# Moving a layer norm's statistics into the stage ahead of it, and re-ordering the projection stage of an attention layer

## The chip, the cores and the metric

The kernel runs on one core of a Trainium2 chip. The metric is the device time of one execution, in microseconds (us).

## The reference, cut to what matters

An image of 256 channels and 64 x 64 pixels goes through two layers. Layer 0 normalizes groups of channels, computes a linear attention whose sums over windows are taken with an integral image (window sizes 64, 32 and 16), projects it and adds the input. Layer 1 sees the 4096 pixels as tokens of 256 channels: softmax attention with 8 heads over normalized tokens, then a mixture of experts (top 2 of 8).

```python
x = x + L0_conv(_gn(x), Wq, Wk, Wv, Wout, bout)
t = _to_tokens(x)                                   # 4096 x 256
t = t + L1_attn(_ln_t(t), w_qkv, b_qkv, w_out, b_out)
t = t + L1_ffn(_ln_t(t), Wr, br, ln_g, ln_b, W1, b1, W2, b2)

def _ln_t(v, eps=1e-5):                             # the norm that the change moves
    m = mean(v, -1); s = var(v, -1)
    return (v - m) / sqrt(s + eps)
```

The change concerns the end of layer 0, and of layer 1 the first norm and the products q, k and v.

## The kernel before

All tokens stay on the chip in `t`, 32 tiles of 128 tokens by 256 channels, with 8 more columns for the router. The image is cut into 8 strips (`NCH` = 8), each of `NB` = 4 tiles: strip or chunk c holds the tiles 4c to 4c+3.

**The end of layer 0.** The function `attend` runs for each half of the channels (g = 0, 1), and in it for each window in the order (1, 0, 2). The last window of the second half (w = 2, r = 1) goes over the 8 strips. A strip has up to six steps, alternately 384 and 512 columns wide. A step makes scores for four heads on TensorE (L738) into four PSUM banks out of six that rotate (tag `sc`, `bufs=6`). `masked` then multiplies them by masks into SBUF: VectorE does it straight from PSUM (L568), and for head 1, in every other step for head 3 too, ScalarE copies (L564) and GpSimd multiplies (L568). Two steps later the masked scores go against v (L754). A score bank comes free when VectorE's multiply or ScalarE's copy has read it, and the next step's scores of heads 2 and 3 go into the banks that this step's heads 0 and 1 had. After a strip's last step VectorE multiplies the sum by the reciprocals (L769), and two steps later, in the third step of the next strip, `projection` makes the output product (L641) in two of the rotating banks and VectorE adds it to `t` (L645), two tiles at a time. With that add the strip's four tiles of layer 1's input are final.

**The start of layer 1.** The weights `wqkv` come by DMA on SyncE's queue (L863), the bias rows on ScalarE's (L866, L867). For a chunk the kernel takes the statistics of four tiles (`stats`: L801, L802), adds epsilon and takes the root (`begin`: L806 on VectorE, L807 on ScalarE), inverts it (`end`: L810), normalizes each tile to `hn` (L926), turns it on TensorE (L816) and copies it to `act` (`to_channels`, L817). Then come 8 products for q and k, 512 wide (L947), on each of which VectorE adds the bias (L951) and takes the largest absolute value (L952), and 8 products for v (L958), biased by VectorE (L965) and with the router's columns copied by ScalarE (L966). GpSimd adds the output bias to `t` (L936). The first two chunks' statistics and the small products `biases` and `router` are placed by hand. PSUM has four rotating banks here (`psum("a_ps0", 4)`).

After the last chunk a bound on the scores is worked out from the largest values (L988 to L1003), every engine reads its verdict `tame` (L1004) and branches, and the attention begins with L1074. Each engine runs its own instructions in order; what the order is, a scheduler of the framework decides from the program's order and priorities.

Of the kernel before, what the change touches and what calls it, by code (L numbers as in the profile page):

```python
# [34 lines left out]
NT = N // P  # L35
CH = 512
NCH = N // CH
# [3 lines left out]
NB = IMG // BH  # L41
# [5 lines left out]
NE = 8  # L47
# [5 lines left out]
TAME = 60.0  # L53
# [58 lines left out]
def tile_conv_attn_hybrid(ctx: ExitStack, tc: tile.TileContext, a: dict, out: bass.AP):  # L112
    nc = tc.nc

    const = ctx.enter_context(tc.tile_pool(name="const", bufs=1))
    keep = ctx.enter_context(tc.tile_pool(name="keep", bufs=1))

    def psum(name, bufs):
        return tc.tile_pool(name=name, bufs=bufs, space=PSUM)
# [9 lines left out]
    cst = constants_of("", const)  # L129
    ident = cst["ident"]  # L130
# [5 lines left out]

    wr_sum = keep.tile([P, NE], F32, name="wr_sum")
    act = keep.tile([P, KC, N], F32, name="act")

    def tok(i):  # L140
        return slice(P * i, P * (i + 1))
# [44 lines left out]
    with ExitStack() as phase:  # L186
# [28 lines left out]
        with (  # L215
# [58 lines left out]
            for i in range(0, NCH, 2):  # L274
                for k in range(KC):
# [5 lines left out]
                        op0=ALU.subtract,  # L281
# [311 lines left out]
        def attend(g, work, ps, qk, v, ssum, rec, woT):  # L593
# [34 lines left out]
            for w in windows:  # L628
# [8 lines left out]
                def projection(ix, raw=raw, w=w):  # L637
                    for b in range(0, NB, 2):
                        po = score().rearrange("p (i o) -> p i o", o=C)
                        for i in range(2):  # L640
                            nc.tensor.matmul(  # L641
                                po[:, i, :], raw[:, ix, tok(b + i)], woT[:, w, :], start=True, stop=True
                            )
                        to = t[:, NB * ix + b : NB * ix + b + 2, :C]
                        nc.vector.tensor_add(to, po, to)  # L645

# [140 lines left out]
            with tc.tile_pool(name="c_work", bufs=1) as work, psum("c_ps2", 1) as ps:  # L787
                attend(g, work, ps, *of)

    class Norm:  # L790


        def __init__(self, pool, name):
            self.pool = pool
            self.mv = pool.tile([P, NT, 2], F32, name=f"{name}_mv")
            self.rstd = pool.tile([P, NT], F32, name=f"{name}_rstd")
            self.mean, self.var = self.mv[:, :, 0], self.mv[:, :, 1]

        def stats(self, i):
            st6 = self.pool.tile([P, 6], F32, tag="st6", name="st6", bufs=2)  # L800
            nc.vector.bn_stats(st6, t[:, i, :C])  # L801
            nc.vector.bn_aggr(self.mv[:, i, :], st6)  # L802

        def begin(self, first, last):

            nc.vector.tensor_scalar_add(self.rstd[:, first:last], self.var[:, first:last], 1e-5)  # L806
            nc.scalar.sqrt(self.rstd[:, first:last], self.rstd[:, first:last])  # L807

        def end(self, first, last):
            nc.vector.reciprocal(self.rstd[:, first:last], self.rstd[:, first:last])  # L810

    def to_channels(src, dst, ps):

        tp = ps.tile([P, CH], F32, tag="mm", name="ps_mm")
        for k in range(KC):
            last = nc.tensor.transpose(tp[:, tok(k)], src[:, tok(k)], ident)  # L816
        nc.scalar.copy(dst, tp[:, :C].rearrange("p (k n) -> p k n", k=KC))  # L817
        return last
# [20 lines left out]
    with ExitStack() as phase:  # L839
# [15 lines left out]
        with (  # L855
            tc.tile_pool(name="a_in", bufs=1) as win,
            tc.tile_pool(name="a_ln", bufs=2) as work,
            psum("a_ps0", 4) as ps,
        ):

            wqkv = win.tile([P, KC, 3 * C + NE], F32, name="wqkv")
            wr = wqkv[:, :, 3 * C :]
            nc.sync.dma_start(wqkv[:, :, : 3 * C], a["L1_attn_w_qkv"].rearrange("(k p) o -> p k o", p=P))  # L863
            nc.sync.dma_start(wr, a["L1_ffn_Wr"].rearrange("(k p) e -> p k e", p=P))
            rows6 = win.tile([6, P], F32, name="bias_rows")
            nc.scalar.dma_start(rows6[:4], a["L1_attn_b_qkv"][: 2 * C].rearrange("(m p) -> m p", p=P))  # L866
            nc.scalar.dma_start(rows6[4:], a["L1_attn_b_out"].rearrange("(m p) -> m p", p=P))  # L867
            bo = row_on_all("L1_attn_b_out", C, win)
            bv = win.tile([P, C], F32, name="bv")
            nc.scalar.dma_start(bv, a["L1_attn_b_qkv"][2 * C :].partition_broadcast(P))  # L870
# [4 lines left out]
            def biases():  # L875
                tp = ps.tile([P, CH], F32, tag="mm", name="ps_mm")
                nc.tensor.transpose(tp[:, :6], rows6, ident[:6, :6])
                nc.vector.tensor_copy(bqk, tp[:, :6])
# [30 lines left out]
                        )  # L909
                nc.vector.tensor_copy(wo[:, :, C:], tp[:, : KC * NE].rearrange("p (k e) -> p k e", e=NE))  # L910

            norm = Norm(small, "ln1")

            def begin(c):
                for i in range(NB * c, NB * (c + 1)):
                    norm.stats(i)
                norm.begin(NB * c, NB * (c + 1))

            begin(0)
            for c in range(NCH):  # L920
                if 0 < c < NCH - 1:
                    begin(c + 1)
                norm.end(NB * c, NB * (c + 1))
                for i in range(NB * c, NB * (c + 1)):
                    hn = work.tile([P, C], F32, name="hn", bufs=4)
                    last = nc.vector.tensor_scalar(  # L926
                        hn,
                        t[:, i, :C],
                        norm.mean[:, i : i + 1],
                        norm.rstd[:, i : i + 1],  # L930
                        op0=ALU.subtract,
                        op1=ALU.mult,
                    )
                    turned = to_channels(hn, act[:, :, tok(i)], ps)

                    nc.gpsimd.tensor_add(t[:, i, :C], t[:, i, :C], bo)  # L936
                if c == 0:

                    with tc.issue_after(last.ins), tc.issue_after(turned.ins):
                        biases()  # L940
                        begin(1)
                for s in range(2):
                    for g in range(KC):
                        m = KC * s + g
                        pr = ps.tile([P, CH], F32, tag="mm", name="ps_mm")
                        for k in range(KC):
                            nc.tensor.matmul(  # L947
                                pr, wqkv[:, k, tok(m)], act[:, k, chunk(c)], start=k == 0, stop=k == KC - 1
                            )
                        to = qk[:, s, g, chunk(c)]  # L950
                        nc.vector.tensor_scalar_add(to, pr, bqk[:, m : m + 1])  # L951
                        nc.vector.tensor_reduce(  # L952
                            peak[:, s, g, c : c + 1], to, AX.X, ALU.max, apply_absolute_value=True
                        )
                for i in range(NB * c, NB * (c + 1)):
                    pv = ps.tile([P, CH], F32, tag="mm", name="ps_mm")
                    for k in range(KC):
                        product = nc.tensor.matmul(  # L958
                            pv[:, : C + NE],
                            act[:, k, tok(i)],  # L960
                            wqkv[:, k, 2 * C :],
                            start=k == 0,
                            stop=k == KC - 1,
                        )
                    biased = nc.vector.tensor_add(v[:, i, :], pv[:, :C], bv)  # L965
                    nc.scalar.copy(t[:, i, C:], pv[:, C : C + NE])  # L966
                if c == 0:
                    with tc.issue_after(biased.ins), tc.issue_after(product.ins):
                        router()
                if c == 2:  # L970
                    expert_columns(win, ps)
# [15 lines left out]
            top = small.tile([P, 2, KC], F32, name="top")  # L987
            nc.vector.tensor_reduce(top, peak, AX.X, ALU.max)  # L988
            most = small.tile([P, KC, 4], F32, name="most")
            nc.vector.tensor_mul(  # L990
                most,
                cst["head"].unsqueeze(1).to_broadcast([P, KC, 4]),
                top[:, 0].unsqueeze(2).to_broadcast([P, KC, 4]),
            )
            nc.vector.tensor_mul(most, most, top[:, 1].unsqueeze(2).to_broadcast([P, KC, 4]))
            tp = ps.tile([P, CH], F32, tag="mm", name="ps_mm")
            nc.tensor.matmul(
                tp[:1, : 4 * KC], ones[:, :1], most.rearrange("p g h -> p (g h)"), start=True, stop=True
            )
            bound = small.tile([1, 1], F32, name="bound")  # L1000
            nc.vector.tensor_reduce(bound, tp[:1, : 4 * KC], AX.X, ALU.max)
            tame = small.tile([1, 1], mybir.dt.int32, name="tame")
            nc.vector.tensor_scalar(tame, bound, TAME / C**-0.5, None, op0=ALU.is_le)  # L1003
        tame = nc.values_load(tame[:1, :1], min_val=0, max_val=1)  # L1004

        attnT = act
# [639 lines left out]
```

## Time and profile before

| what | value |
|---|---|
| time before | 2807.0 us, median of 3 runs (2806.38 to 2809.07) |
| the profiled execution | 2808.7 us, its span 2806.9 us |
| TensorE busy, share of the span | 2661.7 us, 95% |
| VectorE, ScalarE, GpSimd busy | 1879.4, 1489.9, 813.6 us |
| the last window of layer 0, second half | about 907 to 1003.3 us of the span |
| norm, q, k and v of layer 1 | 1003.3 to 1113.7 us of the span |

The span is what the profiler saw from the first to the last instruction; the execution's time is 1.8 us longer. The profile is of one execution. Times in the views are microseconds from the span's start. TensorE's matmuls are pipelined, so "busy" on it means that some matmul was in flight.

### The profile page before, as it was taken

To read this page: it belongs to the slowest core of one execution; us is meant where nothing else is said; L and a number is where in the kernel's file an instruction comes from. 1 tells how busy PE (TensorE), PEld (TensorE's weight loads), DVE (VectorE), ACT (ScalarE), POOL (GpSimd) and SP (SyncE) were. 2 spreads that over 40 slices of the span, in tenths; PEclk is the share of its full clock that TensorE was granted. 3 is DMA by queue.
4 is the path that set the end of the run, shared out by engine and by line. 5 is a ranking of instruction groups with operands and counts; after the bars stand their busy time and mean duration, and the time that the engine had idled before them with its cause. 6 is when DMAs were issued, how large, how long until landed. Compare 5 with 4: busy or idle time off the path is not lost.

```text
span 2806.9 us, 72020 instructions
## 1 busy us (share of the span) xinstructions
PE 2661.7 (95%) x31078; PEld 1217.1 (43%) x31078; DVE 1879.4 (67%) x2476; ACT 1489.9 (53%) x2060; POOL 813.6 (29%) x914
## 2 busy tenths in 40 slices
PE   6889999998999989999999999999999689999996
PEld 5454336645433655111212121222222168888884
DVE  6758688575878886888888888888888721111114
ACT  3222323222232312999898989898999622222222
POOL 2057777305777831000000000000000022222220
PEclk9999999999999999999999999999999879999997
DMA  5000000000000000555555555555555356656665
GB/s 143 6 23 26 10 28 21 8 0 23 28 7 32 17 21 1 106 110 121 109 116 110 117 110 120 110 111 110 118 108 120 86 186 214 197 196 197 205 216 190
DMA packets 120044, 264.97 MB, mean 94 GB/s; under 512 B 20099, under 2 KB 81129, under 8 KB 105637
## 3 DMA queue, kind: packets, MB, share of 16 engines
q0 software_dynamic: 22368, 133.18, 22.4%
q1 hardware_dynamic: 90168, 118.15, 12.9%
q10 hardware_dynamic: 7180, 8.93, 0.9%
q8 instruction: 248, 4.06, 0.6%
q14 instruction: 80, 0.65, 0.1%
HBM read 126.76 MB, written 18.12 MB: 52 GB/s over the span
## 4 chain that ended last, share of the span: by engine, by line
PE 92%; DVE 3%; issue 2%; DMA 2%; ACT 1%; POOL 0%; SPq 0%; ACTq 0%; DVEq 0%; POOLq 0%
PE ps_three L1074 18%; PE ps_acc L1033 18%; PE ps_hp L1552 9%; PE ps_yp L1561 8%; PE ps_sc L738 8%; PE ps_acc L754 7%; PE ps_sc L641 3%; PE ps_sc L665 3%; PE ps_acc L696 3%; PE ps_mm L947 2%; PE ps_two L329 2%; PE ps_two L362 2%; PE ps_two L443 1%; PE ps_acc L684 1%; PE ps_mm L958 1%
## 5 line engine op out<-in xcount | busy, mean ns | idle before, releaser
L1074 PE MATMUL ps_three<-qk 32*64 32x512 f32 x6144 | 564.0, 613 | 3.3 <-DVE t L983 1.8
L1074 PE MATMUL ps_one<-qk 32*64 32x512 f32 x2048 | 557.5, 613 | 1.4 <-ACT pe L1083 1.4
L1105 DVE TENSOR_TENSOR act<-act,pe 128x2048 f32<-128x2048 f32 x195 | 446.8, 2292 | 97.2 <-ACT pe L1086 62.9
L564 ACT COPY sm<-ps_sc 128x384 f32<-128x384 f32 (+3 forms) x454 | 218.5, 511 | 531.0 <-PE ps_sc L738 345.8
L1086 ACT ACTIVATE pe<-ps_three 128x1536 f32<-128x1536 f32 x330 | 476.9, 1445 | 0.0
L568 DVE TENSOR_TENSOR sm<-ps_sc,mask 128x512 f32<-128x512 f32 (+3 forms) x740 | 340.1, 519 | 70.2 <-PE ps_sc L738 66.9
L568 POOL TENSOR_TENSOR sm<-sm,mask 128x192 f32<-128x192 f32 (+3 forms) x428 | 350.1, 848 | 111.9 <-ACT sm L564 111.5
L1105 DVE TENSOR_TENSOR act<-act 128x2048 f32<-128x2048 f32 x150 | 343.8, 2292 | 55.7 <-ACT act L1086 42.5
L1094 POOL DMA_DIRECT2D pe<-pe x108 | 93.1, 862 | 953.7 <-ACT pe L1086 652.2
L1033 PE MATMUL ps_acc<-pe,v 128*32 128x512 f32 x2640 | 352.4, 606 | 0.0
L1555 ACT ACTIVATE hid<-ps_hp,cols 128x256 f32<-128x256 f32 (+1 forms) x288 | 133.2, 462 | 360.2 <-PE ps_hp L1552 359.1
L1074 PEld LDWEIGHTS ps_three<-qk 32*64 32x64 f32 x6144 | 112.7, 130 | 416.5 <-ACT pe L1083 243.2
L1086 ACT ACTIVATE act<-ps_three 128x1536 f32<-128x1536 f32 x182 | 263.2, 1446 | 0.0
L1552 PE MATMUL ps_hp<-xe,w 128*128 128x256 f32 (+1 forms) x1152 | 246.8, 371 | 0.0
L1561 PE MATMUL ps_yp<-w,hid 128*128 128x256 f32 x1088 | 240.8, 379 | 0.0
L738 PE MATMUL ps_sc<-qk 32*64 32x384 f32 (+3 forms) x3584 | 232.4, 458 | 0.0
L1083 ACT ACTIVATE pe<-ps_one 128x512 f32<-128x512 f32 x330 | 197.4, 598 | 59.4 <-PE ps_one L1074 35.7
L568 POOL TENSOR_TENSOR sm<-sm,ycut 128x384 f32<-128x384 f32 (+4 forms) x146 | 147.5, 1031 | 252.3 <-ACT sm L564 252.0
L1552 PEld LDWEIGHTS ps_hp<-xe,w 128*128 128x128 f32 x1152 | 201.2, 190 | 39.5 <-ACT hid L1555 5.3
L1561 PEld LDWEIGHTS ps_yp<-w,hid 128*128 128x128 f32 x1088 | 204.2, 190 | 26.4
L754 PE MATMUL ps_acc<-sm,v 128*32 128x256 f32 (+3 forms) x2688 | 213.2, 419 | 0.1
L1531 DVE TENSOR_SCALAR xe<-ps_tp,cols 128x256 f32<-128x256 f32 (+1 forms) x72 | 34.8, 525 | 238.9 <-PE ps_tp L1527 217.2
(253 smaller groups left out, 3006.8 us busy)
## 6 DMA issues: line engine op xcount, KB each, us to landing
pe<-pe POOLq DMA_DIRECT2D x108, 1024.0 KB, 7.4
w<-in_L_ffn_W SPq DMA_DIRECT2D x72, 1024.0 KB
by<-recs SPq DMA_DIRECT2D x48, 256.0 KB
b<-in_L_ffn_b SPq DMA_DIRECT2D x36, 128.0 KB
rows<-in_x SPq DMA_DIRECT2D x16, 256.0 KB
zrows<-act SPq DMA_DIRECT2D x4, 1024.0 KB
y<-yrows ACTq DMA_DIRECT2D x8, 512.0 KB
y<-yrows SPq DMA_DIRECT2D x8, 512.0 KB
```

The source lines that it names most:

```text
L564: nc.scalar.copy(sm[:, :used], sc[:, :used])
L568: done = engine.tensor_mul(to, of, mk.unsqueeze(1).to_broadcast(list(to.shape)))
L738: nc.tensor.matmul(scs[h][u : u + rows, at : at + n], kT[hs[h], P * i + u : P * i + u + rows], qT[hs[h], CH * ix + CELL * c0 : CH * ix + C ...
L754: nc.tensor.matmul(acc[hs[h], CELL * c0 : CELL * c1], v[:, i, hs[h]], sms[h][:, at : at + n], start=not begun[0], stop=last and at == plac ...
L1033: nc.tensor.matmul(to[D * hd : D * (hd + 1), :], lhsT(hd), rhs(hd), start=start, stop=stop, skip_group_check=True,)
L1074: nc.tensor.matmul(to[CELL * u : CELL * (u + 1), :], qk[hs, 1, g, P * i + CELL * u : P * i + CELL * (u + 1)], qk[hs, 0, g, chunk(qc)], sta ...
L1083: first = nc.scalar.activation(head(pe, 0), one, AF.Exp, scale=C**-0.5)
L1086: nc.scalar.activation(pe[:, CH:], three.rearrange("p h n -> p (h n)"), AF.Exp, scale=C**-0.5).ins
L1105: latest[:] = [nc.vector.tensor_add(total, total, weights_of[r, i]).ins]
L1552: nc.tensor.matmul(hp[:, :n], w1[:, k, tok(m)], x_now[:, k, :n], start=k == 0, stop=k == KC - 1)
L1555: nc.scalar.activation(hid[:, m, :n], hp[:, :n], AF.Gelu, bias=cols[:, m : m + 1])
L1561: nc.tensor.matmul(yp, hid[:, m, tok(j)], w2[:, m, :], start=m == 0, stop=m == NH - 1)
```

## The change

It does four things.

1. The class `Norm` moves up, and `norm1` is made before layer 0. In the last window of the second half, `projection` of the strips 0 to 6 takes the statistics of each tile right after the add to `t`, and calls `begin` for its chunk and `end` for the one before. After strip 6 chunk 0 is also normalized, into columns of `act` that layer 0 has done with (`first_rows`). Chunk 7's statistics are taken in layer 1.
2. In layer 1 each chunk is normalized and turned (`turn(c + 1)`) between the q, k products and the v products of the chunk before it; `turn(0)` runs at the start. PSUM has eight rotating banks instead of four.
3. ScalarE adds the biases of q and k (`activation` with `Identity`) where VectorE did. A small `Exp` is called on ScalarE ahead of the loop. The two bias rows' DMAs go ahead of the weights on SyncE's queue instead of following `wo` on ScalarE's.
4. The bound (`bounds`) is worked out before the last two tiles' v products instead of after them.

```diff
+    norm1 = Norm(keep, "ln1")
+    first_rows = lambda i: act[:, KC - 1, N - C * (i + 1) : N - C * i]
...
                         to = t[:, NB * ix + b : NB * ix + b + 2, :C]
                         nc.vector.tensor_add(to, po, to)
+                        if g == KC - 1 and w == windows[-1] and ix < NCH - 1:
+                            for i in range(2):
+                                norm1.stats(NB * ix + b + i)
+                    if g == KC - 1 and w == windows[-1] and ix < NCH - 1:
+                        if ix:
+                            norm1.end(NB * (ix - 1), NB * ix)
+                        norm1.begin(NB * ix, NB * (ix + 1))
+                        if ix == NCH - 2:
+                            for i in range(NB):
+                                norm1.apply(first_rows(i), i)
...
-            psum("a_ps0", 4) as ps,
+            psum("a_ps0", 8) as ps,
...
+            nc.sync.dma_start(rows6[:4], a["L1_attn_b_qkv"][: 2 * C].rearrange("(m p) -> m p", p=P))
+            nc.sync.dma_start(rows6[4:], a["L1_attn_b_out"].rearrange("(m p) -> m p", p=P))
             nc.sync.dma_start(wqkv[:, :, : 3 * C], ...)
...
-                        nc.vector.tensor_scalar_add(to, pr, bqk[:, m : m + 1])
+                        nc.scalar.activation(to, pr, AF.Identity, bias=bqk[:, m : m + 1])
...
+            turn(0)
+            biases()
+            root = small.tile([1, 1], F32, name="root")
+            nc.scalar.activation(root, ident[:1, :1], AF.Exp)
+            for c in range(NCH):
+                queries_keys(c)
+                if c + 1 < NCH:
+                    turn(c + 1)
+                if c == 0:
+                    norm.end(NT - 2 * NB, NT - NB)
+                if c == 1:
+                    for i in range(NT - NB, NT):
+                        norm.stats(i)
+                    norm.begin(NT - NB, NT)
+                if c == 2:
+                    norm.end(NT - NB, NT)
                 for i in range(NB * c, NB * (c + 1)):
+                    if i == NT - 2:
+                        bounds()
+                    biased, product = values(i)
```

More of the change, by code (lines that the diff above doesn't have):

```diff
@@ L138, in tile_conv_attn_hybrid, with __init__, stats, begin @@
     act = keep.tile([P, KC, N], F32, name="act")
+    class Norm:
+        def __init__(self, pool, name):
+            self.pool = pool
+            self.mv = pool.tile([P, NT, 2], F32, name=f"{name}_mv")
+            self.rstd = pool.tile([P, NT], F32, name=f"{name}_rstd")
+            self.mean, self.var = self.mv[:, :, 0], self.mv[:, :, 1]
+        def stats(self, i):
+            st6 = self.pool.tile([P, 6], F32, tag="st6", name="st6", bufs=2)
+            nc.vector.bn_stats(st6, t[:, i, :C])
+            nc.vector.bn_aggr(self.mv[:, i, :], st6)
+        def begin(self, first, last):
+            nc.vector.tensor_scalar_add(self.rstd[:, first:last], self.var[:, first:last], 1e-5)
+            nc.scalar.sqrt(self.rstd[:, first:last], self.rstd[:, first:last])
+        def end(self, first, last):
+            nc.vector.reciprocal(self.rstd[:, first:last], self.rstd[:, first:last])
+        def apply(self, to, i):
+            nc.vector.tensor_scalar(
+                to,
+                t[:, i, :C],
+                self.mean[:, i : i + 1],
+                self.rstd[:, i : i + 1],
+                op0=ALU.subtract,
+                op1=ALU.mult,
+            )
+    norm1 = Norm(keep, "ln1")
+    first_rows = lambda i: act[:, KC - 1, N - C * (i + 1) : N - C * i]
     def tok(i):
@@ L788, in tile_conv_attn_hybrid @@
                 attend(g, work, ps, *of)
[L790 to L810, printed above, removed]
     def to_channels(src, dst, ps):
@@ L862, in tile_conv_attn_hybrid @@
             wr = wqkv[:, :, 3 * C :]
+            rows6 = win.tile([6, P], F32, name="bias_rows")
+            nc.sync.dma_start(rows6[:4], a["L1_attn_b_qkv"][: 2 * C].rearrange("(m p) -> m p", p=P))
+            nc.sync.dma_start(rows6[4:], a["L1_attn_b_out"].rearrange("(m p) -> m p", p=P))
             nc.sync.dma_start(wqkv[:, :, : 3 * C], a["L1_attn_w_qkv"].rearrange("(k p) o -> p k o", p=P))
             nc.sync.dma_start(wr, a["L1_ffn_Wr"].rearrange("(k p) e -> p k e", p=P))
[L865 to L867 removed]
             bo = row_on_all("L1_attn_b_out", C, win)
@@ L910, in router, with turn, queries_keys @@
                 nc.vector.tensor_copy(wo[:, :, C:], tp[:, : KC * NE].rearrange("p (k e) -> p k e", e=NE))
-            norm = Norm(small, "ln1")
-            def begin(c):
+            norm = norm1
+            def turn(c):
                 for i in range(NB * c, NB * (c + 1)):
[L916 to L934, printed above, removed]
+                    hn = work.tile([P, C], F32, name="hn", bufs=4) if c else first_rows(i)
+                    if c:
+                        norm.apply(hn, i)
+                    to_channels(hn, act[:, :, tok(i)], ps)
                     nc.gpsimd.tensor_add(t[:, i, :C], t[:, i, :C], bo)
[L937 to L941, printed above, removed]
+            def queries_keys(c):
                 for s in range(2):
@@ L954, in tile_conv_attn_hybrid, with values @@
                         )
-                for i in range(NB * c, NB * (c + 1)):
[L956 to L966, printed above, removed]
+            def values(i):
+                pv = ps.tile([P, CH], F32, tag="mm", name="ps_mm")
+                for k in range(KC):
+                    product = nc.tensor.matmul(
+                        pv[:, : C + NE],
+                        act[:, k, tok(i)],
+                        wqkv[:, k, 2 * C :],
+                        start=k == 0,
+                        stop=k == KC - 1,
+                    )
+                biased = nc.vector.tensor_add(v[:, i, :], pv[:, :C], bv)
+                nc.scalar.copy(t[:, i, C:], pv[:, C : C + NE])
+                return biased, product
@@ new lines, in tile_conv_attn_hybrid, with bounds @@
+            tame = small.tile([1, 1], mybir.dt.int32, name="tame")
+            def bounds():
+                top = small.tile([P, 2, KC], F32, name="top")
+                nc.vector.tensor_reduce(top, peak, AX.X, ALU.max)
+                most = small.tile([P, KC, 4], F32, name="most")
+                nc.vector.tensor_mul(
+                    most,
+                    cst["head"].unsqueeze(1).to_broadcast([P, KC, 4]),
+                    top[:, 0].unsqueeze(2).to_broadcast([P, KC, 4]),
+                )
+                nc.vector.tensor_mul(most, most, top[:, 1].unsqueeze(2).to_broadcast([P, KC, 4]))
+                tp = ps.tile([P, CH], F32, tag="mm", name="ps_mm")
+                nc.tensor.matmul(
+                    tp[:1, : 4 * KC], ones[:, :1], most.rearrange("p g h -> p (g h)"), start=True, stop=True
+                )
+                bound = small.tile([1, 1], F32, name="bound")
+                nc.vector.tensor_reduce(bound, tp[:1, : 4 * KC], AX.X, ALU.max)
+                nc.vector.tensor_scalar(tame, bound, TAME / C**-0.5, None, op0=ALU.is_le)
@@ L983, in tile_conv_attn_hybrid @@
             nc.vector.tensor_add(t[:, :, C:], t[:, :, C:], shift)
[L987 to L1003, printed above, removed]
         tame = nc.values_load(tame[:1, :1], min_val=0, max_val=1)
```

## The prediction

> **What bounds the kernel now.** I read the page first: TensorE is busy for 95% of the span, and the chain that ended last is 92% TensorE. The change touches two stages, so I cut them out: the windows of busy time (time, then PE, PEld, DVE, ACT, POOL, clock, DMA share, GB/s), one strip of layer 0's last window first, then the start of layer 1.
>
> ```profile
> 973.00:986.20 13.20, 13.20 (x208) 8.16 (x203) 10.96 (x25) 4.33 (x10) 10.52 (x15) 1.00 0.01 3
> ...
> 1003.40:1010.00 6.60, 2.23 (x10) 1.72 (x11) 5.79 (x23) 1.69 (x5) 0.12 (x1) 0.80 0.67 208
> 1010.00:1113.60 103.60, 97.78 (x337) 57.50 (x337) 85.53 (x205) 14.98 (x70) 23.61 (x32) 0.98 0.01 1
> ```
>
> A strip of 13.20 us has TensorE busy without a gap, and VectorE has 13.20 - 10.96 = 2.24 us free. Whether added work fits depends on where the free time lies. The timeline of VectorE and TensorE around the add to `t`, and the waits from 960 to 1000 us (total, times, longest):
>
> ```profile
> 982.22 0.69 DVE L645 TENSOR_TENSOR t<-ps_sc,t 128x512 f32<-128x512 f32 x1 [0.25 <-PE ps_sc L641]
> 983.08 0.69 DVE L645 TENSOR_TENSOR t<-ps_sc,t 128x512 f32<-128x512 f32 x1 [0.17 <-PE ps_sc L641]
> 984.13 3.01 DVE L568 TENSOR_TENSOR sm<-ps_sc,mask 128x512 f32<-128x512 f32 x7 [0.36 <-PE ps_sc L738]
> 987.86 0.69 DVE L568 TENSOR_TENSOR sm<-ps_sc,mask 128x512 f32<-128x512 f32 x1 [0.71 <-PE ps_sc L738]
> ```
>
> ```profile
> 985.05 0.93 PE L738 MATMUL ps_sc<-qk 32*128 32x192 f32 x16
> ...
> 986.70 1.20 PE L738 MATMUL ps_sc<-qk 32*128 32x256 f32 x16
> ```
>
> ```profile
> PEld ps_sc L738 <- DVE sm L568: 2.7, 8, 0.4
> ```
>
> The step at 984.13 masks head 0 until 984.13 + 0.68 = 984.81, and that frees the bank which head 2 of the scores at 985.05 needs. TensorE's weight loads already wait for these masks; the slack is 0.2 us. Between the add at 983.08 and the mask VectorE is free for 0.36 us only.
>
> The chain of layer 1, at one chunk's boundary and at the start and end:
>
> ```profile
> 1004.69 4.76 DMA bias_rows<-in_L_attn_b_out
> ...
> 1009.82 9.24 PE ps_mm L947 x16
> ...
> 1059.05 3.56 PE ps_mm L958 x16
> 1062.61 0.23 PE ps_mm L816 x2
> ...
> 1063.31 0.84 ACT act L817 x3
> 1064.15 0.04 issue
> 1064.19 7.13 PE ps_mm L947 x16
> ...
> 1108.15 3.58 PE ps_mm L958 x16
> ...
> 1113.67 0.68 PE ps_three L1074 x6
> ```
>
> From the last v product to the next chunk's first q product pass 1064.19 - 1062.61 = 1.58 us, of which the turning matmuls need about 0.9 (1050.19 to 1051.28 for eight, with the last one's 0.27 of latency); the rest waits for ScalarE's copies.
>
> **Statistics in the strips.** In layer 1 the four tiles of chunk 0 took from 1003.97 (first L801) to 1005.84 (L806): 1.87 us, plus 0.61 where the second add stands between them (0.69 less the overlap of neighbours on VectorE). The built program's order puts add, two tiles' statistics, add, two tiles' statistics ahead of the first mask of the 512-wide step. So that mask starts at 982.91 + 1.87 + 0.61 = 985.39 instead of 984.13, ends at 986.07, and TensorE's head 2 starts 0.05 later (as raw to projection at 1001.28, 1001.33): 986.12 instead of 985.06. TensorE's queue is in order, so everything behind waits: 1.05 us.
>
> The order then has the epsilon add (L806's operation) between this step's masks, and the reciprocal behind them. VectorE: 985.39 + 0.61, epsilon about 0.2, two masks 1.25, reciprocal 0.07, the next step's head 0 in two pieces 0.62: 988.14. TensorE would need that bank at 986.70 + 1.05 = 987.75 and gets it at 988.19: 0.45 more. After that VectorE again waits 0.71 for scores, so the lateness ends there. A strip costs 1.5 us. ScalarE's root stands behind a 512-wide copy and ahead of the next step's copies; it waits for the epsilon add at about 986.2, and the copy behind it is due at 987.1 (986.10 + 1.05), so it delays nobody.
>
> [...] The epsilon add in layer 1:
>
> ```profile
> L806 DVE TENSOR_SCALAR ln_rstd<-ln_mv x9: 155/169/684, 1005.8 to 2224.8; 128x4 f32<-128x4 f32 x8, 128x32 f32<-128x32 f32 x1
> ```
>
> Four elements take 0.169 us, but 0.42 and 0.68 at 1010.49 and 1013.14, while GpSimd's L936 runs. In the strip GpSimd's mask runs from 984.92 to 986.19, so the add at 986.0 waits about 0.2, as counted. [...]
>
> Six strips at 1.5 are 9.0. The four normalizations of chunk 0 stand, in the built order, in the first of these strips, between its masks: 4 x 0.33 = 1.3 free of GpSimd, up to 4 x 0.73 = 2.9 beside it (L926 takes 0.41 alone, 0.73 to 0.89 beside L936); GpSimd is nearly always running there but in pieces of 0.55, so I take 1.6. In the last strip no step follows: the first half of the stall is paid by the last sums and the multiply at 1000.59, 1.2. **Sum: +11.8**, between 8 (statistics interleaving better than they do at 1004) and 15.
>
> **The start of layer 1.** Statistics, root and normalization from 1003.97 to 1007 go, but they hid behind DMAs: the products began at 1009.82, released by the bias rows. Those now go first, and the weights two issues later (about 0.42 each, 1003.39 to 1003.82). All data had moved by 1009.0 (DMA share 0.99 in 1008 to 1009, 0.06 after), so the weights become last, at about 1009.35: **-0.5**, between 0 and -1.5. `wo` and the broadcast rows move up by two issues on ScalarE's queue; `ones` on GpSimd stays put.
>
> The first 16 products take 9.24 instead of 7.13, at half the granted clock (0.50 from 1007.3 to 1014.1, after TensorE's pause from 1003.3). The pause remains, now from 1004.4 to 1009.35 as the turning goes ahead of it: the same 2.1, give or take 1.5. The other half-clock stretch (1119.9 to 1123.4, worth 1.7) may come or not; I count 0.
>
> **The loop.** The gaps between v and the next q products are 4.10 (with the router), 2.23 (with the expert columns) and five of 1.58: 14.2. After it TensorE runs 7 x 0.9 turning + 2.4 router + 0.5 columns = 9.2, unless another engine stops it: **-5.0**. Covers: VectorE per chunk has 4 maxima (0.6), 4 normalizations (up to 0.8 beside GpSimd), 4 adds (0.4) = 7.2 of 11.6; ScalarE 4 biases (0.60, as the 512-wide L1083), 8 copies = 4.7. If one were late, the next boundary would pay 0.7 again. The eight banks let turning run ahead of the copies.
>
> ScalarE's `Exp` gains nothing: the built order has its table load, then a load for chunk 7's root, then a third before the attention's first `Exp`, where it stands now (1.28 at 1115.12). The two added ones, 2 x 1.28 from about 1006.4, end at 1009.2, before the first product at 1011.
>
> [...]
>
> **The bound.** Its matmul waits for the maxima of the last chunk, ready at 1110.7 counted by the old rows (L995 ends 1110.69). TensorE will have finished the first two v tiles at 1108.15 + 1.78 = 1109.93: +0.8. Against that, 1111.72 to 1113.67 (1.95) shrinks, as the verdict is there before the last product; reading and branching (0.95 from 1112.72 to 1113.67) remain. If the read still waits for ScalarE's last copy (1112.37), only 0.3 is won, otherwise 1.0: I take -0.6. **Sum: +0.2.**
>
> **The total.** 11.8 - 0.5 - 5.0 + 0.2 = +6.5. The profiled execution (2808.7, span 2806.9) would become 2815.2; the median of the runs lies 1.7 lower, so 2807.0 + 6.5 = **2813.5 us**. A measurement of this kernel tells about 0.2%, or 5.6 us, from no change: 2801.4 to 2812.6 counts as the same.
>
> **Rivals.**
> - Statistics half hidden: if TensorE keeps going until VectorE's work exceeds a strip (10.96 + 1.87 + 0.35 = 13.18 of 13.20), a strip costs near 0.5, in all 5 with the normalizations: -0.3, 2806.7 us. For it: the total fits. Against: the free time lies after the masks that TensorE waits for. With the forecast's own lower costs (8 and -6) it makes the cases that count as the same: chance 0.35.
> - Statistics wholly hidden and the layer-1 gain full: 0 - 5.3 - 1.7 (no second half-clock stretch) = -7.0, 2800 us, faster. It decides where the mask can start 1.2 us late at no cost, that is, if banks were free earlier than the weight-load waits say. Chance 0.08.
> - [...] It lies in the slower chance, which is 0.57 with the forecast.
> - The change doing nothing would need both stages to be hidden; TensorE's 92% of the chain excludes it.
>
> The range goes from 2806.5, the first rival, to 2818.5, past the third; what is left out is the faster rival and the far end of the stalls.
>
> **What would show it.** Right: strips of 14.7 us, TensorE waiting 1.0 and 0.4 at the next two steps' scores, and longer in the first; no gap but the bound's in the loop; three table loads. Wrong: strips still 13.2 us (the statistics hide), or boundaries that still pay 0.7 (another engine is late).

## The result and the profile after

The changed kernel takes 2814.26 us (median of 16 runs, 2810.36 to 2815.94) where the kernel before takes 2807.15 (16 runs, 2805.60 to 2809.11): a ratio of 1.0023, 95% interval 1.0016 to 1.0031. It is slower, by 7.1 us; 2813.5 was forecast. The profiled execution took 2814.95 us with a span of 2813.2, against 2808.7 and 2806.9 before.

The span is longer by 6.3 us, and four pieces of the timeline make that up: the stretch up to the first projection of the last window -1.76 (914.99 to 913.23; at 142 us the two timelines still agree to 0.01, at 198 they differ by 1.93, in a part of layer 0 that the change leaves as it was), from there to the last projection +13.30 (86.34 to 99.64), from the last projection to the attention's first product -6.14 (112.34 to 106.20), and the rest +0.90. So the change loses 13.3 us in layer 0 and wins back 6.1 in layer 1.

The windows of busy time, with the columns as before: the first strip with statistics, an ordinary one, the wait at layer 1's start, and from its first product to the attention.

```profile
913.23:931.70 18.47, 15.95 (x205) 9.37 (x201) 15.13 (x39) 4.55 (x11) 10.63 (x16) 0.91 0.04 16
975.45:990.03 14.58, 14.24 (x204) 8.72 (x201) 12.84 (x35) 4.54 (x11) 10.51 (x16) 1.00 0.01 3
1014.90:1021.30 6.40, 1.33 (x10) 1.07 (x10) 3.22 (x14) 4.17 (x8) 0.30 (x2) 0.87 0.74 216
1021.30:1119.10 97.80, 95.77 (x342) 57.75 (x343) 47.70 (x101) 35.22 (x95) 23.48 (x32) 0.97 0.01 1
```

An ordinary strip takes 14.58 us instead of 13.21, with VectorE busy for 12.84 of them: there are 1.74 us of free time on VectorE, and TensorE waits all the same. Where, the timeline of the two engines shows (VectorE first):

```profile
976.62 0.69 DVE L680 TENSOR_TENSOR t<-ps_sc,t 128x512 f32<-128x512 f32 x1 [0.25 <-PE ps_sc L676]
977.34 0.75 DVE L151 BATCH_NORM_STATS2 st<-t 128x6 f32<-128x256 f32 x2
978.09 0.66 DVE L680 TENSOR_TENSOR t<-ps_sc,t 128x512 f32<-128x512 f32 x1
978.78 0.76 DVE L151 BATCH_NORM_STATS2 st<-t 128x6 f32<-128x256 f32 x2
979.67 0.66 DVE L603 TENSOR_TENSOR sm<-ps_sc,mask 128x512 f32<-128x512 f32 x1
980.25 0.36 DVE L156 TENSOR_SCALAR ln_rstd<-ln_mv 128x4 f32<-128x4 f32 x1
980.52 1.28 DVE L603 TENSOR_TENSOR sm<-ps_sc,mask 128x512 f32<-128x512 f32 x2
```

```profile
979.45 0.59 PE L783 MATMUL ps_sc<-qk 32*128 32x192 f32 x4
980.38 0.92 PE L783 MATMUL ps_sc<-qk 32*128 32x192 f32 x12 [0.34 <-DVE sm L603]
982.02 1.65 PE L783 MATMUL ps_sc<-qk 32*128 32x256 f32 x16
```

The first mask (979.67) starts 3.05 us after the first add; before it was 1.91 (982.22 to 984.13). The scores of the step behind it break off and go on at 980.38. They break off after 4 of 16 records; the trace has two records for each of a step's eight matmuls, so heads 0 and 1 have run, and head 2 waits for its bank, as forecast. From the start of these scores to that of the next products, which come behind them in TensorE's order, pass 1.78 us (to 981.23) where it was 0.86. The step after that takes 1.58 us to 983.60 instead of 1.13. That is 0.92 + 0.45 = 1.37 us a strip, and TensorE has no other gap in it.

Layer 1 on the chain of work that ended last (start, time, what): the start, one chunk, the bound.

```profile
1015.59 5.53 DMA wqkv<-in_L_attn_w_qkv
...
1021.25 9.68 PE ps_mm L952 x16
...
1069.14 3.56 PE ps_mm L964 x16
1072.70 6.87 PE ps_mm L952 x16
1079.57 0.87 PE ps_mm L839 x8
...
1113.51 0.70 ACT qk L956
...
1116.33 1.99 PE ps_mm L964 x8
```

A chunk is now TensorE alone, 6.87 + 0.87 + 3.56 = 11.30 us, where it was 12.27. Only the start (a DMA) and the bound (ScalarE and VectorE, 1113.51 to 1116.33) are left to others. (The "16 products" of q and k are records too: the code has eight matmuls a chunk, two for each of four outputs, and the bias is added once for each output.)

### The profile page after: what moved, and what is told of

Read it like the earlier page. It is cut to its first block, busy times and chain, and to the rows that moved or that the text cites. A ratio compares the mean times of both kernels' runs of the same rounds, so it can differ in the third digit from the quotient of the medians.

```text
span 2813.2 us, 71995 instructions
## 1 busy us (share of the span) xinstructions
PE 2668.4 (95%) x31078; PEld 1220.3 (43%) x31078; DVE 1856.9 (66%) x2444; ACT 1514.7 (54%) x2095; POOL 812.3 (29%) x914
## 4 chain that ended last, share of the span: by engine, by line
PE 91%; DVE 4%; issue 2%; DMA 1%; SPq 1%; ACT 0%; POOL 0%; DVEq 0%; POOLq 0%; ACTq 0%
PE ps_three L1102 18%; PE ps_acc L1061 18%; PE ps_hp L1580 9%; PE ps_yp L1589 8%; PE ps_sc L783 7%; PE ps_acc L799 7%; PE ps_sc L710 3%; PE ps_acc L741 3%; PE ps_sc L676 3%; PE ps_mm L952 2%; PE ps_two L364 2%; PE ps_two L397 2%; PE ps_two L478 1%; PE ps_acc L729 1%; PE ps_three L1039 1%
## 5 line engine op out<-in xcount | busy, mean ns | idle before, releaser
L783 PE MATMUL ps_sc<-qk 32*64 32x384 f32 (+3 forms) x3584 | 239.5, 459 | 4.2 <-DVE sm L603 4.2
L1061 PE MATMUL ps_acc<-act,v 128*32 128x512 f32 x1456 | 193.9, 604 | 0.0
```

The source lines that it names most:

```text
L783: nc.tensor.matmul(scs[h][u : u + rows, at : at + n], kT[hs[h], P * i + u : P * i + u + rows], qT[hs[h], CH * ix + CELL * c0 : CH * ix + C ...
L1061: nc.tensor.matmul(to[D * hd : D * (hd + 1), :], lhsT(hd), rhs(hd), start=start, stop=stop, skip_group_check=True,)
```

## The experiments

My theory: the 13.3 us are lost because of *where* the statistics stand in a strip, the 6.1 are won by the order of turning and products alone, and the two add up. Rivals: VectorE's *sum* of work in a strip is what costs; layer 1 gains only because its loop has lost the statistics; the four-element epsilon add beside GpSimd is the main cost. Ratios are to the kernel before, run on the same chip in the same job; its medians were 2808.94, 2809.42, 2810.57 and 2806.08 us in the four jobs. "Layer 1" below is the time from the last projection's start to the attention's first product: 112.34 us before, 106.20 after. (The first expectation counts it from that projection's end: 104.2 us after the change.)

### Taking the two halves apart

**The new layer 1 alone.** The strips' lines go, and the statistics are taken in layer 1. The small `Exp` ahead of the loop goes too.

```diff
-                        if g == KC - 1 and w == windows[-1] and ix < NCH - 1:
-                            ... (statistics, epsilon, root, reciprocal, normalization in projection)
-            norm = norm1
+            norm = Norm(small, "ln1")
...
+            begin(0)                      # stats of 4 tiles, epsilon, root
+            norm.end(0, NB)
             turn(0)
             biases()
-            root = small.tile([1, 1], F32, name="root")
-            nc.scalar.activation(root, ident[:1, :1], AF.Exp)
+            begin(1)
             for c in range(NCH):
                 queries_keys(c)
                 if c + 1 < NCH:
+                    norm.end(NB * (c + 1), NB * (c + 2))
                     turn(c + 1)
+                if c + 2 < NCH:
+                    begin(c + 2)
```

> The strips keep no statistics; they are taken in layer 1 (chunk 0's at its start, each later chunk's two chunks ahead), everything else as changed. My theory (the strips cost 13.3 us because of where the statistics stand, the new order of layer 1 gains 6.1 us whatever becomes of them): strips back at 13.2 us, layer 1 from the last projection to the attention's first product at about 104.5 us as after the change, 2807.2 - 6 = 2801 us (2799 to 2803). Rival (the gain in layer 1 is there only because VectorE has no statistics left in the loop): 28 tiles at 0.46 us come back into the chunks, the boundary waits 0.7 us again, layer 1 takes 109 us or more, about 2806 us.

Measured: 2802.13 us, ratio 0.9976 (0.9967 to 0.9985). The strips are back at 13.21 us and layer 1 takes 106.11, with all 32 tiles' statistics in it. The loop has room for them: VectorE was busy for 85.53 of 103.60 us in it before, and for 47.70 of 97.80 after the change. The rival is out, and this half of the change is a gain by itself.

**The statistics in the strips alone**, on the kernel before:

```diff
+                        ... (the statistics and the rest of the lines in projection, as in the change)
...
-            begin(0)
...
-                if 0 < c < NCH - 1:
-                    begin(c + 1)
+                if c == NCH - 2:
+                    begin(c + 1)
-                norm.end(NB * c, NB * (c + 1))
+                if c >= NCH - 2:
+                    norm.end(NB * c, NB * (c + 1))
```

> The kernel before with the first part of the change alone: statistics in the strips, chunk 0 normalized there, layer 1 otherwise in its old order. My theory: the strips lose 13.3 us and layer 1 wins nothing from it, as its loop waited for TensorE and its start for DMAs: 2807.2 + 13.3 = 2820 us (2818 to 2822). Rival (the loop was held up by the statistics on VectorE): the boundaries of 1.58 us shrink, up to 7 x 0.7 = 4.9 us come back, 2815 us.

Measured: 2822.87 us, ratio 1.0051 (1.0037 to 1.0065). From the first to the last projection 99.63 us, as after the change; layer 1 takes 113.05 us, no less than before. Its boundaries still wait for ScalarE's copies (chain of waits):

```profile
1052.32 0.84 ACT act L840 x3
1053.16 0.04 issue
1053.20 7.13 PE ps_mm L963 x16
```

So taking the statistics out of the loop brought nothing there. -6.8 and +13.9 us give +7.1, which is what both together measured; with intervals of 2.5 and 4 us to each side, that they agree so closely is luck.

### What in a strip costs

**Without the normalizations.** The four of chunk 0 wait for the last projection's add.

```diff
-                        if ix == NCH - 2:
-                            for i in range(NB):
-                                norm1.apply(first_rows(i), i)
...
-                    if c:
+                    with tc.issue_after(added[0]) if not c else nullcontext():
                         norm.apply(hn, i)
```

> As changed, but the four normalizations of chunk 0 wait for the last projection's add instead of standing in the first strip. My theory: their 2.3 us there caused the 2.2 us stall and the drop of the granted clock behind it; the first strip becomes like the other five (14.6 instead of 18.5 us), the clock stays at 1.00 through it, and the normalizations hide behind the weights' DMA at layer 1's start: 2814.3 - 3.9 = 2810.4 us. Rival (the drop of the clock has nothing to do with the stall): it comes all the same, and the kernel wins 2.2 us at most: 2812 us or more.

Measured: 2811.42 us, ratio 1.0008 (0.9999 to 1.0017). The time alone, between the two expectations, doesn't decide; the trace does. The first strip in the windows of busy time (the eighth column is the granted clock):

```profile
913.63:928.22 14.59, 14.25 (x205) 8.72 (x201) 12.85 (x35) 4.55 (x11) 10.53 (x16) 1.00 0.06 20
```

It is now like the others, with the clock at 1.00. What the normalizations had done there is in the timeline of the changed kernel:

```profile
919.70 2.31 DVE L163 TENSOR_SCALAR act<-t,ln_mv,ln_rstd 128x256 f32<-128x256 f32 x4
```

```profile
922.69 1.13 PE L783 MATMUL ps_sc<-qk 32*128 32x256 f32 x12 [2.18 <-DVE sm L603]
923.75 1.71 PE L799 MATMUL ps_acc<-sm,v 128*32 128x256 f32 x16
925.39 1.66 PE L783 MATMUL ps_sc<-qk 32*128 32x192 f32 x16
```

TensorE waits for 2.18 us, and then its products take 1.71 and 1.66 us where they took 1.07 and 0.93: the granted clock (the eighth column) is 0.50 from 924.03 to 927.45.

```profile
924.03:927.45 3.42, 3.42 (x40) 1.83 (x36) 1.68 (x5) 0.68 (x2) 1.27 (x1) 0.50 0.03 7
```

Without the wait the stretch doesn't come. The other runs say the same: all six profiled executions with the normalizations in the first strip have it there, behind a wait of 1.63 to 2.19 us, and none of the eight without them has.

**The same statistics at other places.** Two tiles each ahead of the two 512-wide steps whose first mask came after 0.71 us of idle time, behind the mask before; normalizations as in the last run.

```diff
+                def first_two(ix):
+                    with tc.issue_after(latest[0]):
+                        for i in range(2):
+                            norm1.stats(NB * ix + i)
+                def other_two(ix):
+                    with tc.issue_after(latest[0]):
+                        ... (the other two, and the reciprocal of the strip before)
+                    norm1.begin(NB * ix, NB * (ix + 1))
...
-                                chores.extend([lambda: None, lambda: projection(ix)])
+                                chores.extend([lambda: None, lambda: projection(ix), lambda: None,
+                                    lambda: first_two(ix), lambda: None, lambda: other_two(ix)])
```

> As changed, with the same statistics in the same strips, but two tiles each ahead of the two 512-wide steps before whose first mask VectorE has 0.71 us to spare, and chunk 0 normalized at layer 1's start. My theory (place, not sum): two tiles take 0.9 us there, of which 0.7 is idle time and about 0.2 slack, a strip takes 13.2 to 13.6 us, and the kernel 2814.3 - 3.9 - 5 to 7 - 1 = 2802 to 2805 us. Rival (VectorE's work in a strip, 10.96 + 2.2 = 13.2 us, leaves no room wherever it stands): strips stay at 14.6 us, 2810 us as in the run without the normalizations.

Measured: 2805.17 us, ratio 0.9983 (0.9974 to 0.9992). One strip in the windows of busy time, then VectorE's timeline in it, then TensorE's:

```profile
981.73:995.27 13.54, 13.54 (x204) 8.46 (x201) 12.81 (x35) 4.43 (x10) 10.54 (x16) 1.00 0.01 1
```

```profile
987.75 0.74 DVE L151 BATCH_NORM_STATS2 st<-t 128x6 f32<-128x256 f32 x2
988.41 0.30 DVE L152 BATCH_NORM_AGGREGATE ln_mv<-st 128x2 f32<-128x6 f32 x2
988.63 2.99 DVE L603 TENSOR_TENSOR sm<-ps_sc,mask 128x512 f32<-128x512 f32 x7
...
992.53 0.30 DVE L156 TENSOR_SCALAR ln_rstd<-ln_mv 128x4 f32<-128x4 f32 x1
992.75 1.87 DVE L603 TENSOR_TENSOR sm<-ps_sc,mask 128x512 f32<-128x512 f32 x3
```

```profile
993.30 1.22 PE L788 MATMUL ps_sc<-qk 32*128 32x192 f32 x16
```

VectorE does the same work (12.81 against 12.84 us), and a strip takes 13.54 us instead of 14.58. The first pair of tiles costs nothing. The second pair has the epsilon add and the reciprocal beside it, and the scores behind it take 1.22 us instead of 0.93: that is the 0.3 that is left. Place decides, not the sum: TensorE hardly waits in a strip in which VectorE is 95% busy.

**The epsilon in the root.** ScalarE adds it as the bias of its square root.

```diff
+    eps = ... (one column, 1e-5)
...
-                        norm1.begin(NB * ix, NB * (ix + 1))
+                        cut = slice(NB * ix, NB * (ix + 1))
+                        nc.scalar.activation(norm1.rstd[:, cut], norm1.var[:, cut], AF.Sqrt, bias=eps)
```

> As changed, but the epsilon is added inside ScalarE's root (as its bias), so that the strips hold no four-element add on VectorE, and the reciprocal stands between the masks instead of behind them. My theory: the second, 0.45 us stall of a strip was this add (0.36 us, of it 0.2 a wait beside GpSimd); without it a strip takes 14.2 us instead of 14.58, 6 x 0.35 = 2 us less: 2812 us. Rival: the reciprocal now waits for ScalarE's root in VectorE's queue with two masks behind it, and the root stands behind a 512-wide copy: the stall stays or grows, strips of 14.6 us or more, 2814 us or more.

Measured: 2813.57 us, ratio 1.0011 (1.0001 to 1.0021). Strips of 14.31 us, between the two expectations:

```profile
979.28 1.14 PE L786 MATMUL ps_sc<-qk 32*128 32x192 f32 x12 [0.34 <-DVE sm L605]
980.35 0.86 PE L802 MATMUL ps_acc<-sm,v 128*32 128x192 f32 x16
981.14 1.16 PE L786 MATMUL ps_sc<-qk 32*128 32x256 f32 x16
```

The second stall is gone (1.16 against 1.65 us), but the reciprocal, which now stands between the masks, adds 0.22 to the first (1.14 against 0.92): 0.27 us net. So the add was worth the second stall, about a third of the 1.37 us, and not the main cost. How much of it is due to GpSimd, this run doesn't separate.

### What in layer 1 gains

**The bound behind the v products**, and **VectorE adding the q and k biases**, each alone undone in the changed kernel:

```diff
-                    if i == NT - 2:
-                        bounds()
...
             nc.vector.tensor_add(t[:, :, C:], t[:, :, C:], shift)
+            bounds()
```

> As changed, but the bound on the scores stands behind the last v product again. My theory: the 1.1 us stall between the v pairs goes and the gap between the last v product and the attention's first product grows from 0.73 to about 1.95 us: 0.1 to 0.3 us slower, not to be told from the changed kernel (2814.5 us). Rival (the early bound is worth the 1.2 us): 2815.5 us, with the stall between the v pairs staying for another reason.

```diff
-                        nc.scalar.activation(to, pr, AF.Identity, bias=bqk[:, m : m + 1])
+                        nc.vector.tensor_scalar_add(to, pr, bqk[:, m : m + 1])
```

> As changed, but VectorE adds the q and k biases again. My theory: with the eight banks and the chunk turned ahead nobody waits for the engine that empties the banks; a chunk stays at 11.30 us with its 16 products at 6.87, and the maxima of the last chunk, which need the bias add on the same engine, come up to 1 us later or earlier at the bound: 2813.5 to 2815.5 us. Rival (ScalarE's part made the products shorter and the boundary free): chunks of 11.6 to 12.3 us, 2817 to 2821 us.

Measured: 2813.98 us, ratio 1.0018 (1.0008 to 1.0027), and 2814.54 us, ratio 1.0022 (1.0012 to 1.0031). Layer 1 takes 106.19 and 106.18 us, against 106.20, and with VectorE's biases a chunk is as long as after the change (from one chunk's first v product to the next one's 11.31 us in both). For the bound, the end of TensorE's timeline in the changed kernel, and below it the attention's first products with the bound behind:

```profile
1116.13 0.19 PE L988 MATMUL ps_mm<-most,ones 128*1 128x8 f32 x2 [0.88 <-DVE most L986]
1116.26 2.05 PE L964 MATMUL ps_mm<-wqkv,act 128*128 128x264 f32 x8
1119.07 0.68 PE L1102 MATMUL ps_three<-qk 32*64 32x512 f32 x6 [0.76 <-ACT t L972]
```

```profile
1119.88 0.68 PE L1101 MATMUL ps_three<-qk 32*64 32x512 f32 x6 [1.86 <-DVE t L1029]
```

A wait of 0.88 ahead of the bound's matmul, which was not there, and one of 0.76 instead of 1.86 behind: the wait was moved, not hidden. Neither edit changes the time by anything that these intervals can tell.

**The turning behind the v products**, with all else as changed:

```diff
                 queries_keys(c)
-                if c + 1 < NCH:
-                    turn(c + 1)
...
+                if c + 1 < NCH:
+                    with tc.issue_after(product.ins):
+                        turn(c + 1)
```

> As changed, but a chunk is turned behind its predecessor's v products on TensorE, as in the kernel before. My theory: each of seven boundaries again waits for ScalarE's copies, 0.7 us, and the 16 products behind it show 7.13 instead of 6.87 us: 7 x 0.97 = 6.8 us slower, 2821 us, so nearly all of layer 1's gain is this order. Rival (the eight banks and ScalarE's bias adds carry the gain): chunks stay below 11.8 us, 2817 us or less.

Measured: 2819.15 us, ratio 1.0037 (1.0023 to 1.0051). By the time alone that lies between the two expectations: 4.6 and 5.2 us above the last two runs, which are of the same job and as long as the change. The trace decides, and 6.1 us lie within the interval: layer 1 takes 112.35 us, to 0.01 that of the kernel before, and a chunk 12.27 (1062.80 to 1075.07, TensorE's timeline):

```profile
1062.80 7.13 PE L952 MATMUL ps_mm<-act,wqkv 128*128 128x512 f32 x16 [0.70 <-ACT act L840]
...
1075.07 7.13 PE L952 MATMUL ps_mm<-act,wqkv 128*128 128x512 f32 x16 [0.70 <-ACT act L840]
```

The time shows less because in this profiled execution no half-clock stretch came at the attention's start: from the attention's first product to the end it took 1691.5 us, against 1694.1 after the change.

Without this one order of instructions nothing of layer 1's gain is left, though the eight banks, ScalarE's bias adds and the early bound are all there. Whether the order would gain as much with four banks, no run shows.

### A version that beats both

**The Exp table loaded early.** The run with the statistics in layer 1, with the Exp of one element in chunk 6:

```diff
+                if c == NCH - 2:
+                    root = small.tile([1, 1], F32, name="root")
+                    nc.scalar.activation(root, ident[:1, :1], AF.Exp)
```

> The run with the statistics in layer 1, and the Exp table loaded in chunk 6, behind the last root, instead of at the attention's start. My theory: every root of the loop is done by chunk 5, Identity and Copy need no table of their own, so the 1.28 us load ahead of the attention's first Exp goes for good: 8.1 us below the kernel before instead of 6.8, 2800.8 us beside 2808.9. Rival (another engine ends last at the attention's start, or ScalarE's copies force the table out): no more than the 6.8 of the first run.

Measured: 2807.30 us, ratio 0.9992 (0.9983 to 1.0001): worse than without it. Nothing held the Exp back, and the framework's scheduler put it at layer 1's start (ScalarE's timeline):

```profile
1005.58 1.28 ACT L1003 ACT_TABLE_LOAD   x1 [6.95 <-DVE ln_mv L152]
1006.87 0.20 ACT L1003 ACTIVATE root<-cst 1x1 f32<-1x1 f32 x1
1007.09 1.28 ACT L157 ACT_TABLE_LOAD   x1
```

The root that chunk 0 waits for stands behind two loads, and the first product comes at 1012.87, 8.97 us after the last projection's end (1007.49 and 6.30 in the run without). With a tie to the last root the same line does what it should:

```diff
+                    with tc.issue_after(norm.rooted):
                         nc.scalar.activation(root, ident[:1, :1], AF.Exp)
```

> The statistics in layer 1, with the Exp of one element now tied behind the last root, so that the Exp table is loaded once, in the loop. My theory (in the run before it stood at layer 1's start, where its load and the root's reload sat ahead of the copies the first products wait for): the start is as in the run with the statistics in layer 1 (106.1 us from the last projection to the attention's first product), and the 1.28 us load at the attention's first Exp is gone: 8 us below the kernel before. Rival (the attention's start waits for another engine just as long): 6.8 us below, as without it.

Measured: 2798.94 us, ratio 0.9970 (0.9959 to 0.9982). No load is left at the attention's start; the only one in layer 1 stands in the loop, and the Identity and Copy instructions between it and the attention's `Exp` at 1110.90 brought none (ScalarE's timeline):

```profile
1033.74 1.28 ACT L1004 ACT_TABLE_LOAD   x1
```

From the attention's first product to the end of the span pass 1690.4 us instead of 1693.2. Not all of these 2.8 us are the load's. Five other runs have the load at the attention's start but no half-clock stretch there, and take 1691.5 to 1691.9 us. So the load is worth 1.1 to 1.6 us. The rest, 1.2 to 1.7, fits the half-clock stretch of 3.41 us that the kernel before has there and this run has not; whether the tie keeps it away, no run shows. In the profiled execution the router's copies came 0.8 us later than in the first run, TensorE waited 1.25 us for them, and the granted clock was 0.50 from 1025.03 to 1031.85; layer 1 took 109.15 us there, 3.0 more than in the first run (TensorE's timeline):

```profile
1024.03 0.36 PE L916 MATMUL ps_mm<-wqkv,woT 128*128 128x8 f32 x2 [1.25 <-DVE woT L912]
```

The median is 7.1 below the kernel before, the ratio says 8.4, and with these intervals it can't be told from the run without the Exp.

**And the start.** Chunk 0's statistics alone in one strip, at the places of the spread run; the weights' q columns as a DMA of their own ahead of everything, `wo` last. First with the Exp untied, then tied:

```diff
-            nc.sync.dma_start(rows6[:4], ...)
-            nc.sync.dma_start(rows6[4:], ...)
-            nc.sync.dma_start(wqkv[:, :, : 3 * C], a["L1_attn_w_qkv"]...)
+            for n in range(3):
+                nc.sync.dma_start(wqkv[:, :, C * n : C * (n + 1)], weights_of[:, :, C * n : C * (n + 1)])
+                if not n:
+                    ... (the two bias rows)
             nc.sync.dma_start(wr, ...)
+            nc.sync.dma_start(wo[:, :, :C], ...)
... (chunk 0's statistics in one strip, the others in the loop, the Exp in chunk 6)
```

> That run, and two things for layer 1's start: chunk 0's statistics alone stand in a strip of layer 0, at the places of the spread run (one strip 0.3 us longer), with the normalization between the last multiply and the last adds; and the q columns of the weights come as a DMA of their own ahead of the bias rows, wo behind all of them on the same queue. My theory (the start waits for the 1 MB of weights, 6.3 us from the last projection to the first product): a third of the bytes suffices, the first product comes about 4 us after the last projection, 2 us earlier, and the half-clock stretch, if TensorE's pause is shorter, may shrink: 10 to 13 us below the kernel before, 2796 to 2799 us beside 2808.9. Rival (the DMAs have a fixed delay, or the k weights now come late): no gain over the run with the Exp table, 2801 us.

> The same tie in the run with chunk 0's statistics in one strip and the weights in three DMAs. My theory: without two table loads at layer 1's start the copies of chunk 0 end at 1008, the products start with the q columns' landing at 1010.1 instead of 1010.7, the first chunks are not held up, and the attention's load goes: 103.7 - 0.6 = 103.1 us from the last projection to the attention, 1.3 less behind it, 11 us below the kernel before (9.2 in the run before, less 1.9). Rival (the start waits for DMAs and the attention's start for another engine): 9 us below.

Measured: 2801.36 us, ratio 0.9965 (0.9952 to 0.9979), 9.2 us below the kernel before and short of the 10 to 13 expected, and 2794.83 us, ratio **0.9956 (0.9943 to 0.9970)**, 11.3 us below the kernel before. TensorE's first products of the latter:

```profile
1007.75 9.96 PE L966 MATMUL ps_mm<-act,wqkv 128*128 128x512 f32 x16 [0.71 <-DMA wqkv<-in_L_attn_w_qkv]
```

They come 4.94 us after the last projection's end, against 6.39 after the change: 1.4 us are won, not 2, since the q columns, a third of the weights, land 4.74 us after their issue (1002.88 to 1007.62), where the whole took 5.53. The half-clock stretch did not shrink (9.96 us for the 16 products), and layer 1 takes 105.04 us instead of the 103.1 expected. Behind the attention's first product pass 1690.2 us, as in the run with the tied Exp; as there, part of that is a half-clock stretch that did not come. In the untied run the stretch at layer 1's start did shrink (8.80 us for the 16 products), with a start at 4.77, so that this too is left to chance.

## Why the prediction was right, by its own steps

The total held (+6.5 against +7.1 by the medians and +6.3 by the spans), partly because two errors go against each other: layer 0 lost 1.5 us more than forecast, layer 1 won 0.8 more. That they nearly cancel is luck. The spans also hold -1.76 and +0.90 outside the change.

| term | forecast | measured |
|---|---|---|
| an ordinary strip: two stalls | 1.05 + 0.45 | 0.92 + 0.45 |
| six strips | +9.0 | +8.2 (6 x 1.37) |
| normalizations in the first strip | +1.6 (1.3 to 2.9) | +3.9 (5.26 - 1.37) |
| last strip | +1.2 | +1.18 |
| layer 0 | +11.8 (8 to 15) | +13.3 |
| layer 1's first product | -0.5 (0 to -1.5) | -0.11 |
| its first 16 products (9.24, then 9.68) | 0 (+-1.5) | +0.44 |
| loop | -5.0 | -6.5 |
| bound and attention's start | +0.2 | +0.06 |
| layer 1 | -5.3 | -6.1 |

- **The strips.** The mechanism was the one forecast: statistics ahead of a mask that frees a bank, then the epsilon add between the next masks. The first stall is a little shorter, since the mask came 1.14 us later than before and not 1.26. The spread run shows it: the same work costs 0.33 us a strip elsewhere.
- **The normalizations** are the mis-sized term. Three of the four took 0.675 us (the last 0.52), 2.31 in all, nearer the upper bound (2.9, beside GpSimd) than the 1.6 I took. And the drop of the clock behind the wait, 1.6 us, was in no step. GpSimd's masks ran from 919.48 to 921.86, beside these normalizations; layer 1's 28 have a median of 0.41 us, with 0.92 as the longest. Why they take longer beside GpSimd, no run shows.
- **The loop.** I read a boundary's cost as 1.58 us against 0.9. From the start of the turning to that of the next products the old boundary is 1.74 (1062.45 to 1064.19) and the new one 0.88 (1079.40 to 1080.28), and the 16 products of a chunk are done 0.1 us sooner when nothing is waited for ahead of them (6.97 against 6.86 from their start to that of what follows): 0.97 a chunk instead of 0.68.
- **The start.** The weights became last, as forecast, but landed 5.53 us after their issue: 6.26 after the last projection's end instead of 6.0.
- **The table loads** are three, as forecast, and gain nothing. The `ACTIVATE` at the attention's start comes 0.02 us behind its load (1120.52 + 1.28, then 1121.82), and in the run with the untied Exp a load starts 0.02 us behind the `ACTIVATE` ahead of it (1006.87 + 0.20, then 1007.09): in these rows a switch is the 1.28 us of its load and a gap of 0.02.
- **The rivals.** Half hidden: refuted by strips at 14.58 us with VectorE at 12.84. Wholly hidden: its layer-1 half is what the first run measured (2802), its strips are not. The third, 2817 us, has the epsilon add 0.5 us longer in each of seven strips (0.68 - 0.17, by L806 in the kernel before): it took 0.36 us, 0.19 more than the 0.17 of before and about what was counted (0.2 of wait), not 0.5 more. The second half-clock stretch of the attention's start came as before (3.41 us from 1125.42), worth nothing either way.

## What to carry to other kernels

Free time on an engine is worth what the wait behind it allows: put new work behind the instruction that frees a buffer, not ahead of it, and look for the idle time just before the next one; here 12.8 us of work cost 1.4 us a strip at one place and 0.3 at another. A change of several parts is worth taking apart, since one part (the turning ahead of the v products) held the gain, one all the loss, and two did nothing that could be measured. And an instruction that depends on nothing is put where a scheduler likes; tie it to what it has to follow.

## What the hardware showed that I had not expected

A single wait of TensorE of 2.18 us was followed, 1.3 us after its end, by 3.41 us at half clock (1.6 us lost); waits of 0.34 us in the other strips were not. In the run with the tied Exp a wait of 1.25 us, among small products, was followed by 6.83 us at half clock; one of 0.45 us at the same place in the first run was not. The stretches around the change are 3.41 us long (924.03 to 927.45) or twice that (1025.03 to 1031.85).

The length of a wait alone doesn't decide. In the changed kernel's trace TensorE also waited 1.94 us (up to 166.89) and 1.68 us (up to 657.91), and the clock stayed at 1.00 from 160 to 180 and from 650 to 670. What else decides, no run here shows. So a stall near 2 us can cost nearly twice its length, as it did in the first strip (2.18 + 1.6 us), and times of this kernel differ with where these stretches fall. From the attention's first product to the end, with the table load there, the runs took 1691.5 to 1691.9 us without a stretch at the attention's start, 1693.1 to 1694.1 with one of 3.41 us and 1694.6 to 1695.2 with one of 6.83 us.
